# Gate and up of a shared expert: 32 products of 256 columns against 56 of 128 columns in the two-by-two scheme of the routed bases

## The chip, the cores and the metric

The kernel runs on one core of one Trainium2 chip. The metric is device time in microseconds (us). One execution was also taken with the hardware profiler; the page and the views of the trace that are quoted below all come from that one execution.

## The reference, cut to what matters

Eight batches of 256 tokens and 512 channels go through a layer norm and a windowed attention, and then, after a second layer norm (`xt`), through this block:

```python
gate = (xt @ w_gate).reshape(T, K, I)          # K = 8 bases, I = 256
up = (xt @ w_up).reshape(T, K, I)
basis = silu(gate) * up
...                                            # router: top 4 of 128 experts
mixed = einsum('tek,tki->tei', mix_sel, basis)
down = einsum('tei,ih->teh', mixed, w_down)
out = einsum('teh,te->th', down, coeff)
shared = silu(xt @ shared_w_gate) * (xt @ shared_w_up) @ shared_w_down
out = out + shared                             # shared_w_gate, shared_w_up: 512 x 512
```

Everything is f32. The routed part comes to a weighted sum over the 8 bases with one weight per token and basis, followed by one product with `w_down`. The shared expert has 512 hidden units, as many as two bases, and no weight per token.

## The kernel before

**One list per engine.** The kernel is one program of Python generators (`project`, `attention`, `tail`, `feed_forward`), each working on one batch. A planner, `run` (L1110), always resumes the generator with the lowest due time. What a generator issues between two yields goes to the engines' queues in that order, and the number that it yields, times a length divided by its `total`, is its next due time. So the yields only fix the order in which instructions stand in each engine's queue; the time comes from the chip. Due times are counted in batches: `feed_forward(b)` runs from b to b+1 with `total=73.2` (L1146), `attention(b+2)` begins at b+0.8 (L1141), and `tail(b+1, 1)`, the last part of the next batch's attention and its router, starts at about b+0.64.

**Routed bases: seven products.** For each basis k gate and up are computed together. The tokens are split in two halves of 128 (t = 0, 1) and the 512 channels in two halves of 256, and instead of eight products of blocks seven are made of sums of blocks (Winograd's form of Strassen's scheme). The sums of tokens, `sT`, are four vector additions per batch in `token_sums` (L717), called by the tail of that batch as soon as its `hT` (the normed tokens, transposed) is whole. The sums of weights are made in batch 0 by `sub` (L838), stored to DRAM scratch by `keep` (L846) and loaded in place of the originals from batch 1 on. `block(k, m, dst)` (L887) is one of the seven products: two matmul calls, tokens as the stationary operand (128x128), weights moving with 256 columns.

**One basis in the queues.** `one_and_five` (4 calls), then `first_tile` of the basis before (an addition `up0` on VectorE, a tanh on ScalarE, `silu2` on VectorE), `four` of the basis before (2 calls), copies `u` and `m5` on ScalarE, `mix_product` (VectorE, with an addition on GpSimd), `seven_and_six` (4 calls), `second_gate` of the basis before (addition `gate1`, tanh, `silu2`), `two_and_three` (4 calls), and `keep_seven` (a copy on ScalarE, an addition on VectorE, two on GpSimd). Three PSUM banks rotate among all of these (`next_bank`, L79).

**Shared expert.** After basis 7 (L1007 to L1057) gate and up are made as plain products with the weights standing still: for each of four blocks `ic` of 128 hidden units, 4 calls for gate and 4 for up, 256 tokens moving, into one bank `ps`; then a tanh, `silu2` and one product give `shT[:, ic, :]`, transposed as the down product needs it. The 8 calls of L1025 for `ic` = 0 are interleaved with what is left of basis 7; after `ic` = 2 the mixture is transposed (`pm`, four transposes) and copied to `mT` on ScalarE (L1060).

**Down products.** 12 calls of 512 columns: four with the lower half of the shared hidden units (L1071), and per tile of tokens two with `mT` and two with the upper half (L1088); then `x = pd * tg + x` on VectorE (L1090) and a store.

**Loads.** All loads of weights are issued by SyncE (SP), whose queue is in order. `after(i, g)` (L340) asks for the piece two ahead once a buffer has been read. The pieces 8 and 9 are the shared weights, 8 loads of 256 KB in place of a base's 7. The tag `w30` holds the moving weights of product 7, and at the end of a batch the lower half of `sw_down` (`load_down`, L336); the `w30` pieces of the next batch's first two bases are loaded after the products of L1071 (L1075). The upper half of `sw_down` stays in SBUF as `later["sd"]` (L261). `diagonals` (L444) issues 16 DMAs per batch through SP.

In f32 each matmul call leaves two LDWEIGHTS rows (PEld) and two MATMUL rows (PE) in the trace, so the 256 calls of L1025 show as x512.

Of the kernel before, what the change touches and what calls it, by code (L numbers as in the profile page):

```python
# [9 lines left out]
F32 = mybir.dt.float32  # L10
I32 = mybir.dt.int32
AF = mybir.ActivationFunctionType
ALU = mybir.AluOpType
AX = mybir.AxisListType

P = 128
# [13 lines left out]
SI = 512  # L30
# [6 lines left out]
def gated_block(  # L37
# [79 lines left out]
    def weight(src, rows, cols, name, eng):  # L117
        t = const.tile([P, rows // P, cols], F32, tag=name, name=name)
        eng.dma_start(t, src.rearrange("(c p) n -> p c n", p=P))
        return t  # L120
# [131 lines left out]
    def first_weights():  # L252

        for k in (2, 3, 0, 1):
            for g in range(1, 5):
                load_gu(k, g)
            if k == 2:
                yield 1.0
                later["wd"] = weight(w_down, I, HID, "wd", nc.sync)

                later["sd"] = weight(sw_down[SI // 2 :], SI // 2, HID, "sd", nc.sync)  # L261
            if k == 3:
                yield 2.0
                yield from first_sums(2)
                yield 1.0
                yield from first_sums(3)
        yield 3.0
        yield from first_sums(0)
        yield 1.0
        yield from first_sums(1)  # L270
# [16 lines left out]
    def coefficients(amp, escale):  # L287
# [21 lines left out]
    HALF = HID // 2  # L309
    scratch = {  # L310
        (k, g): sums.tile([P, 2, I], F32, tag=f"s{k}_{g}", name=f"s{k}_{g}")
        for k in range(NK)
        for g in range(1, 5)
    }

# [2 lines left out]
    def load_gu(i, g):  # L318

        b, k = divmod(i, PIECES)  # L320
        if b >= B or (k >= NK and g > 2):
            return
        wgu[i, g] = ts = [
            two.tile([P, 2, I], F32, tag=f"w{g}{j}", name=f"w{g}{j}_{i}")
            for j in range(1 if g == 3 else 2)
        ]
        if k >= NK:
            for half in range(2):
                nc.sync.dma_start(ts[half], (sw_gate if g == 1 else sw_up)[k - NK, half])
            return  # L330
        if g != 3 or k not in summed:
            nc.sync.dma_start(ts[0], (w_gate, w_gate, w_up, w_up)[g - 1][k, int(g in (2, 4))])
        if k in summed:
            nc.sync.dma_start(ts[-1], scratch[k, g])

# [4 lines left out]
    def after(i, g):  # L340

        b, k = divmod(i, PIECES)
        if g < 3:
            load_gu(i + 2, g)
        elif k < NK - 2:
            load_gu(i + 2, g)
        elif g == 3:
            load_down(b, k - (NK - 2))
        else:
            load_gu((b + 1) * PIECES + k - NK + 2, g)  # L350

# [360 lines left out]

    sides = {}

    def token_sums(b, hT):  # L717


        sT = one.tile([P, NC, T], F32, tag="sT", name=f"sT_{b}").rearrange(  # L720
            "p s (c n) -> p s c n", n=P
        )
        a11, a12 = hT[:, : NC // 2, :P], hT[:, NC // 2 :, :P]
        a21, a22 = hT[:, : NC // 2, P:], hT[:, NC // 2 :, P:]
        nc.vector.tensor_add(sT[:, 0], a21, a22)
        nc.vector.tensor_sub(sT[:, 1], sT[:, 0], a11)
        nc.vector.tensor_sub(sT[:, 2], a11, a21)
        nc.vector.tensor_sub(sT[:, 3], a12, sT[:, 1])
        return sT

    def tail(b, t, oT):
# [47 lines left out]
        give_bank()  # L779
        yield 2.5  # L780
        turned.add((b, t))
        if t == NT - 1:
            sides[b] = token_sums(b, hT)


        yield from take_bank()
# [76 lines left out]
    def feed_forward(b):  # L863
# [23 lines left out]
        def block(k, m, dst, first=False):  # L887
            g, j = weights_of[m]
            w = wgu[b * PIECES + k, g][j]
            for c in range(NC // 2):  # L890
                nc.tensor.matmul(  # L891
                    dst, lhsT=sides_of[m][c], rhs=w[:, c, :],
                    start=(first and c == 0), stop=(c == NC // 2 - 1), skip_group_check=True,
                )

# [58 lines left out]
        def mix_product(k, t):  # L956

            th, up = ths.pop((k, t)), tiles.pop(("m7" if t else "up0", k))
            nc.vector.scalar_tensor_tensor(  # L959
                out=th if k else mixed[t], in0=th, scalar=coef[b, t][:, k : k + 1], in1=up,  # L960
                op0=ALU.mult, op1=ALU.mult,
            )
            if k:
                nc.gpsimd.tensor_add(mixed[t], mixed[t], th)  # L964

        for k in range(NK):
            late = b == 0 and k > 3
            more = b == 0 and 3 < k + 1 < NK  # L970
            one_and_five(k)
            if late:
                keep(k, 3)
# [30 lines left out]
                keep(k + 1, 1)  # L1004


        i = b * PIECES + NK  # L1007
        shT = one.tile([P, NSI, T], F32, tag="shT", name=f"shT_{b}")

        def act(ic, pg):  # L1010
            th = tanh(pg[:, 0, :], f"sth_{b}_{ic}")
            yield 0.7
            silu2(th, pg[:, 0, :])
            nc.vector.scalar_tensor_tensor(
                out=shT[:, ic, :], in0=th, scalar=0.5, in1=pg[:, 1, :],
                op0=ALU.mult, op1=ALU.mult,
            )

        last = None
        for ic in range(NSI):  # L1020
            pg = next_bank(f"ps_{b}_{ic}")
            for j in range(2):
                w = wgu[i + ic // 2, j + 1]
                for c in range(NC):
                    nc.tensor.matmul(  # L1025
                        pg[:, j, :], lhsT=w[c // 2][:, c % 2, ic % 2 * P : (ic % 2 + 1) * P],
                        rhs=hT[:, c, :], start=(c == 0), stop=(c == NC - 1),
                    )
                if ic == 0:

                    if j == 0:
                        yield from first_tile(NK - 1)
                        yield 1.13
                        four(NK - 1)
                        mix_product(NK - 1, 0)
                        yield 0.86
                    else:
                        yield from second_gate(NK - 1)
                        yield 0.63
            if ic % 2:  # L1040
                for g in range(1, 3):
                    after(i + ic // 2, g)
            cost = 3.46 if ic > 0 else 0.0
            if last is not None:
                yield from act(*last)
                cost -= 0.7
            last = ic, pg
            if ic == 1:
                mix_product(NK - 1, 1)
            yield cost  # L1050
            if ic == 2:

                pm = next_bank(f"pm_{b}").rearrange("p t (j n) -> p t j n", j=2)
                for t in range(NT):
                    for j in range(2):
                        nc.tensor.transpose(
                            pm[:, t, j, :], mixed[t][:, j * P : (j + 1) * P], ident  # L1057
                        )
        mT = one.tile([P, NT, 2, P], F32, tag="mT", name=f"mT_{b}")
        nc.scalar.copy(mT, pm)  # L1060
        late = act(*last)


        down = [wgu[b, "sd", ic].rearrange("p c n -> p (c n)") for ic in range(NSI // 2)]
        down += [later["sd"][:, ic, :] for ic in range(NSI // 2)]
        pds = []
        for t in range(NT):
            po = next_bank(f"pd_{b}_{t}").rearrange("p a n -> p (a n)")
            pds.append(po)
            for ic in range(NSI // 2):  # L1070
                nc.tensor.matmul(  # L1071
                    po, lhsT=shT[:, ic, t * P : (t + 1) * P], rhs=down[ic],
                    start=(ic == 0), stop=False,
                )
        for k in range(2):  # L1075
            load_gu((b + 1) * PIECES + k, 3)
        cost = 3.46
        for step in late:
            yield step
            cost -= step  # L1080
        yield cost
        for t, po in enumerate(pds):
            inner = [(mT[:, t, j, :], later["wd"][:, j, :]) for j in range(2)]
            inner += [
                (shT[:, ic, t * P : (t + 1) * P], down[ic]) for ic in range(NSI // 2, NSI)
            ]
            for j, (lhsT, rhs) in enumerate(inner):
                nc.tensor.matmul(po, lhsT=lhsT, rhs=rhs, start=False, stop=(j == len(inner) - 1))  # L1088
            yield 3.46
            nc.vector.scalar_tensor_tensor(  # L1090
                out=xt[:, t, :], in0=po, scalar=tg[:, 1:2], in1=xt[:, t, :],
                op0=ALU.mult, op1=ALU.add,
            )
            nc.sync.dma_start(out[b, t * P : (t + 1) * P, :], xt[:, t, :])
        stored.add(b)


# [24 lines left out]
    with tc.manual_schedule():  # L1122
# [14 lines left out]
        for b in range(B):  # L1137
# [5 lines left out]
                at = float(b)  # L1143
            else:
                start(attention(1), 0.74, at=max(at, FIRST), total=74.1)
            start(feed_forward(b), b + 1.0 - at, at=at, total=73.2)  # L1146
            if b + 2 < B:
                start(project(b + 2), 0.62, at=b + (0.01 if b > 0 else -0.06), total=60.0)
        run(float(B + 1))
# [39 lines left out]
```

## Time and profile before

| what | us |
|---|---|
| median of 3 runs | 1043.92 |
| lowest, highest | 1040.56, 1044.18 |
| profiled execution, its own time | 1039.71 |
| its span, first to last instruction | 1037.9 |

| engine | busy us | share of the span |
|---|---|---|
| PE (TensorE matmul) | 999.2 | 96% |
| PEld (weight loads, beside PE) | 793.6 | 76% |
| DVE (VectorE) | 582.1 | 56% |
| POOL (GpSimd) | 439.7 | 42% |
| ACT (ScalarE) | 420.5 | 41% |

The profiled execution lies 4.2 us under the median of the timed runs and 0.85 us under the fastest of them; 1.8 us of its time lie outside its span. A row of a group gives the mean duration of one instruction; matmuls are pipelined, so the duration of one is longer than its distance to the next. The chain of waits is better for that: it gives for each run of matmuls how long the engine was held. From batch 1 to batch 5 the batches follow each other every 123.6 to 124 us. The DMA engines' mean share over the span is 55.7% for the queue that SP feeds.

### The profile page before, as it was taken

To read this page: it belongs to the slowest core of one execution; us is meant where nothing else is said; L and a number is where in the kernel's file an instruction comes from. 1 tells how busy PE (TensorE), PEld (TensorE's weight loads), DVE (VectorE), ACT (ScalarE), POOL (GpSimd) and SP (SyncE) were. 2 spreads that over 40 slices of the span, in tenths; PEclk is the share of its full clock that TensorE was granted. 3 is DMA by queue.
4 is the path that set the end of the run, shared out by engine and by line. 5 is a ranking of instruction groups with operands and counts; after the bars stand their busy time and mean duration, and the time that the engine had idled before them with its cause. 6 is when DMAs were issued, how large, how long until landed. Compare 5 with 4: busy or idle time off the path is not lost.

```text
span 1037.9 us, 26745 instructions
## 1 busy us (share of the span) xinstructions
PE 999.2 (96%) x10072; PEld 793.6 (76%) x10072; DVE 582.1 (56%) x2185; ACT 420.5 (41%) x1608; POOL 439.7 (42%) x860
## 2 busy tenths in 40 slices
PE   6789989999999999999999999999999999999998
PEld 5657877867788688886878868787788868777885
DVE  1565666747554575536755467544756457754452
ACT  3452554426441464315543256423554136431220
POOL 3666456605542265413644136521454216540340
PEclk9889999999999999999999999999999999999999
DMA  8833964549543693527745386444954368553880
GB/s 254 217 109 115 234 186 150 174 129 283 163 137 111 169 300 123 159 98 191 263 138 157 107 235 217 144 136 125 278 163 144 112 166 258 167 174 120 263 277 20
DMA packets 111104, 180.80 MB, mean 174 GB/s; under 512 B 12160, under 2 KB 34176, under 8 KB 110976
## 3 DMA queue, kind: packets, MB, share of 16 engines
q1 hardware_dynamic: 108480, 176.22, 55.7%
q10 hardware_dynamic: 2112, 1.84, 0.5%
q8 instruction: 79, 1.29, 0.5%
q0 software_dynamic: 384, 1.05, 0.5%
q14 instruction: 49, 0.40, 0.1%
HBM read 149.69 MB, written 12.58 MB: 156 GB/s over the span
## 4 chain that ended last, share of the span: by engine, by line
PE 83%; DVE 8%; ACT 2%; DMA 2%; issue 2%; POOL 1%; SPq 1%; ACTq 0%; POOLq 0%; DVEq 0%
PE m L891 32%; PE ps L1025 10%; PE pq L512 8%; PE sc L645 5%; PE pd L1088 5%; PE po L758 5%; PE sc L576 5%; PE pd L1071 3%; PE pv L532 2%; PE pk L493 2%; DVE pr L589 2%; PE pl L789 1%; DVE pt L623 1%; ACT pr L603 1%; DMA w<-in_L_ffn_w_up 1%
## 5 line engine op out<-in xcount | busy, mean ns | idle before, releaser
L615 POOL TENSOR_SCALAR pr<-pr,rd 128x192 f32<-128x192 f32 (+2 forms) x512 | 206.5, 422 | 271.1 <-DVE rd L612 257.9
L603 ACT ACTIVATE pr<-pr,nm 128x192 f32<-128x192 f32 (+2 forms) x512 | 218.6, 430 | 109.8 <-DVE nm L589 73.8
L891 PE MATMUL m<-w,sT 128*128 128x256 f32 x1024 | 252.7, 381 | 0.1
L589 DVE CUSTOM_DVE_ANT_1 pr<-sc,nbias 128x192 f32<-128x192 f32 (+2 forms) x512 | 153.5, 322 | 122.9 <-PE sc L576 108.7
L891 PEld LDWEIGHTS m<-w,sT 128*128 128x128 f32 x1024 | 194.3, 191 | 27.7 <-issue 1.0
L891 PE MATMUL m<-w,hT 128*128 128x256 f32 x768 | 204.1, 388 | 0.0
L891 PEld LDWEIGHTS m<-w,hT 128*128 128x128 f32 x768 | 139.8, 191 | 24.2 <-issue 5.4
L964 POOL TENSOR_TENSOR mixed<-mixed,th 128x256 f32<-128x256 f32 x112 | 82.0, 732 | 177.3 <-DVE th L959 175.7
L1025 PE MATMUL ps<-hT,w 128*128 128x256 f32 x512 | 117.6, 381 | 0.0
L623 DVE STREAM_TRANSPOSE pt<-pr 128x768 f32<-128x768 f32 (+2 forms) x128 | 111.4, 871 | 3.3 <-POOL prob L798 1.9
L1025 PEld LDWEIGHTS ps<-hT,w 128*128 128x128 f32 x512 | 95.2, 190 | 14.7 <-issue 2.9
L603 ACT ACTIVATION_READ_ACCUMULATOR pr<-pr,nm 128x1 f32 x512 | 97.8, 191 | 0.0
L645 PEld LDWEIGHTS sc<-pt,vbd 64*32 64x32 f32 x5120 | 61.8, 106 | 27.5 <-issue 12.2
L645 PE MATMUL sc<-pt,vbd 64*32 64x96 f32 (+2 forms) x5120 | 70.9, 229 | 7.1 <-DMA vbd<-vpad 3.5
L576 PE MATMUL sc<-kT,qT 32*128 32x192 f32 (+2 forms) x1024 | 67.8, 343 | 6.3 <-DVE nm L589 6.0
L927 POOL TENSOR_TENSOR m<-m,u 128x256 f32<-128x256 f32 x64 | 47.7, 745 | 55.9 <-DVE u L926 47.0
L576 PEld LDWEIGHTS sc<-kT,qT 32*128 32x128 f32 x1024 | 48.2, 188 | 27.6 <-DVE nm L589 9.2
L949 DVE TENSOR_TENSOR gate<-u,m 128x256 f32<-128x256 f32 x64 | 26.4, 413 | 67.5 <-PE m L891 67.5
L854 ACT ACTIVATE th<-m 128x256 f32<-128x256 f32 x64 | 24.7, 386 | 96.6 <-DVE up L937 94.5
L854 ACT ACTIVATE th<-gate 128x256 f32<-128x256 f32 x64 | 26.5, 415 | 87.4 <-DVE gate L949 87.4
L758 PE MATMUL po<-wo,oT 128*128 128x512 f32 x128 | 57.7, 594 | 0.3 <-DVE cf L832 0.3
L512 PE MATMUL pq<-ctT,wq 128*128 128x256 f32 x224 | 54.2, 385 | 2.8 <-ACT kT L500 2.8
(129 smaller groups left out, 1212.8 us busy)
## 6 DMA issues: line engine op xcount, KB each, us to landing
w<-s SPq DMA_DIRECT2D x232, 256.0 KB, 3.3
w<-in_L_ffn_w_gate SPq DMA_DIRECT2D x132, 256.0 KB, 3.1
w<-in_L_ffn_w_up SPq DMA_DIRECT2D x74, 256.0 KB, 4.0
vbd<-vpad SPq DMA_DIRECT2D x120, 128.0 KB, 3.3
s<-w SPq DMA_DIRECT2D x32, 256.0 KB, 3.1
w<-in_L_ffn_shared_w_gate SPq DMA_DIRECT2D x32, 256.0 KB, 3.1
w<-in_L_ffn_shared_w_up SPq DMA_DIRECT2D x32, 256.0 KB, 2.9
ctT<-in_ctx SPq DMA_DIRECT2D x8, 512.0 KB, 5.7
```

Source lines behind the costliest of these rows:

```text
L512: nc.tensor.matmul(pq, lhsT=wq_sb[:, c, g * P : (g + 1) * P], rhs=(ctT if c < NC else xnT)[:, c % NC, :], start=(c == 0), stop=(c == 2 * N ...
L576: nc.tensor.matmul(seen(scs[p][:, j * COLS : (j + 1) * COLS], qb), lhsT=qT[rows, qb].rearrange("p g q -> p (g q)"), rhs=kT[rows, par, :, f ...
L589: nc.vector.tensor_tensor_reduce(out=part, in0=seen(scs[p][:, j * COLS : (j + 1) * COLS], qb0 + j), in1=bass.AP(tensor=bias.tensor, offset ...
L603: nc.scalar.activation(part, part, AF.Exp, bias=nmax, scale=-1.0, accum_out=den)
L615: nc.gpsimd.tensor_scalar(part, part, rden[:, p : p + 1], 1.0, op0=ALU.mult, op1=ALU.mult)
L623: nc.vector.transpose(pt[:, u % 4].rearrange("p c (s k) -> p (c s) k", s=2)[:, :, lo:], pr.rearrange("p c (s k) -> p (c s) k", s=2)[:, :, ...
L645: nc.tensor.matmul(scs[gp][32 * c : 32 * (c + 1), 2 * COLS + lo * Q : 2 * COLS + hi * Q], lhsT=vbd[rows, kb % (P // Q), kb // (P // Q) * 2 ...
L758: nc.tensor.matmul(po, lhsT=oT[:, ch // 2, ch % 2, t * P : (t + 1) * P], rhs=wo_sb[:, ch % 2, ch // 2, :], start=(ch == 0), stop=(ch == 3),)
L891: nc.tensor.matmul(dst, lhsT=sides_of[m][c], rhs=w[:, c, :], start=(first and c == 0), stop=(c == NC // 2 - 1), skip_group_check=True,)
L964: nc.gpsimd.tensor_add(mixed[t], mixed[t], th)
L1025: nc.tensor.matmul(pg[:, j, :], lhsT=w[c // 2][:, c % 2, ic % 2 * P : (ic % 2 + 1) * P], rhs=hT[:, c, :], start=(c == 0), stop=(c == NC - 1),)
L1088: nc.tensor.matmul(po, lhsT=lhsT, rhs=rhs, start=False, stop=(j == len(inner) - 1))
```

## The change

The shared expert's gate and up become two more bases, 8 and 9, in the same seven products, with the roles of the operands exchanged: weights stand still, tokens (or their sums) move with 128 columns, and the result is already transposed. A block is then 4 calls of 128 columns in place of 2 of 256. `mix_product` of these two writes `shT`. Their weight sums are made, stored and loaded as for the other bases. Each hidden block pair of a basis covers `ic` = 2(k-8) and 2(k-8)+1; so `w30` now takes the rows `ic` = 0 and 2 of `sw_down`, and `later["sd"]` the rows 1 and 3. Basis 9 keeps `sT` in use until its `two_and_three`, so `token_sums` of the next batch is asked for twice: by the tail, and by `feed_forward` once `two_and_three(9)` stands in the queue; the later of the two issues it. The down products are ordered anew around what is left of basis 9, and the two `w30` loads for the next batch are issued separately. `total` is 72.9.

```diff
-                later["sd"] = weight(sw_down[SI // 2 :], SI // 2, HID, "sd", nc.sync)
+                later["sd"] = sd = const.tile([P, NSI // 2, HID], F32, tag="sd", name="sd")
+                nc.sync.dma_start(
+                    sd, sw_down.rearrange("(j o p) n -> o p j n", o=2, p=P)[1]
+                )
...
-        for k in range(NK)
+        for k in range(PIECES)
...
-        if k >= NK:
-            for half in range(2):
-                nc.sync.dma_start(ts[half], (sw_gate if g == 1 else sw_up)[k - NK, half])
-            return
         if g != 3 or k not in summed:
-            nc.sync.dma_start(ts[0], (w_gate, w_gate, w_up, w_up)[g - 1][k, int(g in (2, 4))])
+            of_bases, of_shared = ((w_gate, sw_gate), (w_up, sw_up))[(g - 1) // 2]
+            src = of_bases[k] if k < NK else of_shared[k - NK]
+            nc.sync.dma_start(ts[0], src[int(g in (2, 4))])
...
+        if g == 3 and k >= NK:
+            load_down(b, 2 * (k - NK))
+        else:
             load_gu(i + 2, g)
...
+    def token_sums(b):
+        if (b, NT - 1) in turned and (b == 0 or b - 1 in unsided):
+            sides[b] = sums_of_tokens(b, hTs[b])
...
+            if k < NK:
+                for c in range(NC // 2):
...
+                return
+            for ic in range(2):
+                cols = slice(ic * P, (ic + 1) * P)
+                for c in range(NC // 2):
+                    nc.tensor.matmul(
+                        dst[:, cols], lhsT=w[:, c, cols], rhs=sides_of[m][c],
+                        start=(first and ic == c == 0), stop=(c == NC // 2 - 1),
+                        skip_group_check=True,
+                    )
...
+            if k >= NK:
+                nc.vector.scalar_tensor_tensor(
+                    out=shT[:, 2 * (k - NK) : 2 * (k - NK) + 2, t * P : (t + 1) * P],
+                    in0=th.rearrange("p (c n) -> p c n", n=P), scalar=0.5,
+                    in1=up.rearrange("p (c n) -> p c n", n=P), op0=ALU.mult, op1=ALU.mult,
+                )
+                return
...
-        for k in range(NK):
+        for k in range(PIECES):
             late = b == 0 and k > 3
-            more = b == 0 and 3 < k + 1 < NK
+            more = b == 0 and 3 < k + 1 < PIECES
...
+        unsided.add(b)
+        token_sums(b + 1)
+        po0 = next_bank(f"pd_{b}_0").rearrange("p a n -> p (a n)")
+        for ic in range(2):
+            shared(po0, 0, ic, start=(ic == 0), stop=False)
+        yield from first_tile(last)
+        yield 1.13
+        four(last)
+        mix_product(last, 0)
+        yield 0.86
+        pm = next_bank(f"pm_{b}").rearrange("p t (j n) -> p t j n", j=2)
+        for t in range(NT):
+            for j in range(2):
+                nc.tensor.transpose(pm[:, t, j, :], mixed[t][:, j * P : (j + 1) * P], ident)
+        yield from second_gate(last)
+        mT = one.tile([P, NT, 2, P], F32, tag="mT", name=f"mT_{b}")
+        nc.scalar.copy(mT, pm)
+        shared(po0, 0, 3, start=False, stop=False)
+        yield 0.86
+        mix_product(last, 1)
+        for j in range(2):
+            mixture(po0, 0, j)
+        yield 1.73
+        shared(po0, 0, 2, start=False, stop=True)
+        po1 = next_bank(f"pd_{b}_1").rearrange("p a n -> p (a n)")
+        shared(po1, 1, 0, start=True, stop=False)
+        load_gu((b + 1) * PIECES, 3)
+        shared(po1, 1, 1, start=False, stop=False)
+        yield 2.6
+        put(po0, 0)
+        for j in range(2):
+            mixture(po1, 1, j)
+        yield 1.73
+        shared(po1, 1, 2, start=False, stop=False)
+        load_gu((b + 1) * PIECES + 1, 3)
+        shared(po1, 1, 3, start=False, stop=True)
+        yield 2.5
+        put(po1, 1)
...
-            start(feed_forward(b), b + 1.0 - at, at=at, total=73.2)
+            start(feed_forward(b), b + 1.0 - at, at=at, total=72.9)
```

`shared` is one down product of 512 columns with `shT[:, ic, ...]`, `mixture` one with `mT`, `put` the addition to `x` and the store (as L1090 and L1094).

## The prediction, on record before the change was run

> **What bounds the kernel.** I read the page first, then the chain of waits, then the timeline of one late batch. The chain, followed back from the last instruction, is almost all TensorE:
>
> ```profile
> PE 83%; DVE 8%; ACT 2%; DMA 2%; issue 2%; POOL 1%; SPq 1%; ACTq 0%; POOLq 0%; DVEq 0%
> PE m L891 32%; PE ps L1025 10%; PE pq L512 8%; PE sc L645 5%; PE pd L1088 5%; PE po L758 5%; PE sc L576 5%; PE pd L1071 3%; PE pv L532 2%; PE pk L493 2%; DVE pr L589 2%; PE pl L789 1%; DVE pt L623 1%; ACT pr L603 1%; DMA w<-in_L_ffn_w_up 1%
> ```
>
> So a shorter list of matmuls shortens the kernel, as long as no wait takes its place. What a matmul costs is not its mean duration (275 ns with 128 columns, 381 with 256: these overlap) but the time for which the chain is held by a run of them. The chain of waits of one batch (start, length, what, number of rows):
>
> ```profile
> 449.03 1.78 PE pv L532 x16
> ...
> 458.63 3.45 PE ps L1025 x16
> ...
> 470.89 0.89 PE pl L789 x8
> 471.78 3.44 PE pd L1071 x8
> ```
>
> One call leaves two rows. So a call with 256 columns (ps) holds TensorE for 3.45 / 8 = 0.431 us, one with 128 columns and a new stationary operand each time (pv) for 1.78 / 8 = 0.2225 (pl: 0.89 / 4, the same), one with 512 for 0.86. TensorE stands still for only about 1.1 us in a batch of 123.7.
>
> **The products.** Out: 32 calls x 0.431 = 13.80 us per batch. In: 2 bases x 7 products x 4 calls x 0.2225 = 12.46. The 12 down calls and 4 transposes stay. Saved: 1.34 us per batch, 10.7 over eight.
>
> [...]
>
> **Work off the path.** Two bases need on VectorE 2 x 3.1 us (407 + 413 + 414 + 413 + 439 + 2 x 505 ns) in place of 4 x 0.84, on ScalarE 2 x 1.92 in place of 4 x 0.38, on GpSimd 4 x 0.74 in place of nothing: 2.8, 2.3 and 2.9 us more per batch. It falls into the stretch where the shared expert stands now (busy time of PE, PEld, DVE, ACT, POOL; then clock, DMA share, GB/s):
>
> ```profile
> 447.00:455.00 8.00, 8.00 (x63) 7.47 (x53) 1.75 (x4) 1.88 (x6) 0.72 (x1) 1.00 0.32 113
> 455.00:462.00 7.00, 7.00 (x27) 4.65 (x26) 3.56 (x8) 0.38 (x1) 1.27 (x2) 1.00 0.16 49
> 462.00:471.00 9.00, 9.00 (x62) 7.84 (x61) 4.22 (x20) 3.54 (x13) 0.24 (x1) 1.00 0.37 126
> ```
>
> VectorE is busy for 9.5 of 24 us there, ScalarE for 5.8, the DMA engines for a third: hidden, also the 14 loads of 256 KB in place of 8 (1.5 MB more per batch, 3.0 us each to land). In batch 0 the sums of two more bases add 4 x 0.69 us on VectorE, 4 x 1.27 on GpSimd and 8 stores. The nearest row: the sums of bases 0 to 7 (L844) made their engines wait 9 us in all for loads, and TensorE waits for 1.3 us in the last 45 us of that batch. Bounds 0 and 2.6 us (two sums ahead of GpSimd's next work); I take 0.8.
>
> **Waits at the end of a batch.** From the yields and lengths I worked out the order in every queue. For batches 1 to 5, after the last product of `two_and_three(9)`, TensorE has: score (u=0), two shared products, the router's pl, `four(9)`, pm, shared(0,3), mixture, score (u=1), the other down products. VectorE: soften, `up0`, soften, `silu2`, the four token sums (b+0.8309), two softens, mix product, `gate1` (b+0.8536), soften, a reciprocal, the router's maximum rnm; ScalarE: prob (b+0.8602), the tanh of `gate1` (b+0.8605), the copy to `mT`. So the copy now stands behind prob, which waits for rnm, which stands behind `gate1`. Before, the copy came ahead of prob and had 3.44 us of L1071 to hide it. The pieces, as they lie in the batch before the change:
>
> ```profile
> 467.95 0.42 DVE L725 TENSOR_TENSOR sT<-hT 128x256 f32<-128x256 f32 x1
> ...
> 469.42 0.22 DVE L589 CUSTOM_DVE_ANT_1 pr<-sc,nbias 128x64 f32<-128x64 f32 x1
> ...
> 470.35 0.56 ACT L1060 COPY mT<-pm 128x512 f32<-128x512 f32 x1
> ...
> 472.14 0.28 DVE L795 TENSOR_REDUCE rnm<-pl 128x1 f32<-128x128 f32 x1
> ...
> 472.46 0.37 ACT L800 ACTIVATE prob<-pl,rnm 128x128 f32<-128x128 f32 x1 [1.14 <-DVE rnm L795]
> ```
>
> The sums take 469.42 - 467.95 = 1.47 us; rnm to prob is 0.32. Counted from the end of `two_and_three(9)`: TensorE reaches pm at 0.08 + 0.70 + 1.72 + 0.89 + 0.89 = 4.28 and the mixture at 4.28 + 0.44 + 0.86 = 5.58. VectorE: first soften 0.83, `up0` 0.98, soften 1.32; tanh on ScalarE 1.49 to 1.89; `silu2` 1.94, sums 2.28 to 3.75, softens, mix product 4.03, `gate1` 4.5 (`four` ends at 4.28), soften 4.84, reciprocal 5.06, rnm 5.2. ScalarE: prob 5.5, tanh 5.9, `mT` 6.3 to 6.85; the weight load of the mixture takes 0.2. **TensorE waits until 7.1: 1.5 us**, plus 0.1 at shared(0,3). Then `silu2` 6.4, soften, mix product 7.0, the router's top four 7.35 to 9.3 (2.0 us, as from 472.95 to 475.0), and the softens that free the banks of the next score at 9.3 and 9.5: that score, due at 8.8, ends **0.4 us** late. Bounds: with the tanh ahead of prob, 0.5 and nothing; with VectorE one stream transpose (0.97) later, 2.5 and 1.4.
>
> A wait also goes:
>
> ```profile
> 483.62 0.44 PE L576 MATMUL sc<-kT,qT 32*128 32x64 f32 x4
> 484.28 0.98 PE L576 MATMUL sc<-kT,qT 32*128 32x64 f32 x12 [0.22 <-DVE nm L589]
> ```
>
> The last score of a batch stands right behind the router's pc and waits for softens that stand behind its result; the first four rows are held 0.49 us too long. Now two down products (1.72 us) lie between. Nothing of this chain is late next: the softens are done by 15.3 on the scale above, the score comes at 16.4.
>
> Batches 1 to 5: -1.34 - 0.49 + 2.0 = +0.17 each, **+0.9**. Batch 6 has no scores, but the sums and the router's top four (2.05) stand ahead of mix product and `gate1`: shared(0,3) starts at 5.7 instead of 3.1, the mixture at 7.05 instead of 4.0; +3.0 - 1.34, **+1.7**. Batch 7: `four` ends 2.6, `gate1` 3.2, tanh 3.7, copy 4.3, mixture 4.5 instead of 3.9: **-0.7**. Batch 0: tanh ahead of the exponentials, 0.45; with 0.8 for the sums and the saving, **-0.1**. Sum: +1.8 us on the profiled 1039.71, or 1041.5. The median of the runs lies 4.2 higher, so I forecast 1043.92 + 1.8 = **1045.7**: even. A measurement of this kernel tells about 0.5% (5.2 us) from no change.
>
> One thing could make batch 6 dearer. After 2.09 us without work the next four rows took 2.05 us where they take 1.03 elsewhere:
>
> ```profile
> 920.97 0.51 PE L829 MATMUL pc<-mix,selT 128*128 128x8 f32 x2 [2.09 <-ACT selT L824]
> 921.34 2.05 PE L891 MATMUL m<-w,hT 128*128 128x256 f32 x4
> ```
>
> That is half speed, 1.7 us lost in all, once at most. [...]
>
> **The loads through SP.** The `w30` piece of the next batch's basis 0 waits for shared(1,0), and eight of the 16 `vbd` DMAs (10.69 us for 16 rows) now stand before it: SP gets through them by 10.6, shared(1,0) ends at 11.9, the piece lands at 15.3 (3.3 us), and product 7 needs it at 19.0. The second piece, behind the other eight and a store, lands by 21.5 and is needed at 25.2. Slack 3.7 us each: no cost.
>
> **Rivals.**
> - *The waits are hidden* (0.17): ScalarE and VectorE keep ahead, as everywhere else in this trace, where `mT` made TensorE wait 0.3 us in all. Then -10.7 - 5 x 0.5 = -13: 1031. Against it: the order of the queues.
> - *Half hidden* (0.15): 1.0 us per batch in place of 2.0, -1 in batch 6: 1.8 - 5 - 1: 1040.
> - *Slower: the late loads* (0.17). Between batches the DMA engines are busiest (0.92 of the first 12 us of a batch) and `w30` has one buffer per parity. It decides once a piece lands over 3.7 us after my figure, for instance if the `vbd` DMAs wait for the batch's own store or landing doubles. Then product 7 of bases 0 and 1 waits, by 0.7 us if landing goes from 3.3 to 7.7, by 2 if SP is held one product longer: 7 x 0.7 to 7 x 2 on top, 1051 to 1060.
> - *Weight loads bind* (0.03): at 190 ns a row 112 of them are 21.3 us per batch, 7.5 more than before, 1100. pv and pl, which load as often, exclude it nearly.
> - *Even* (0.48): 1040 to 1050.
>
> **How the numbers follow.** Faster by over 0.5%: the hidden case, two thirds of the half hidden, a little of the even: 0.30. Slower: late loads, weight loads, a little of the even: 0.22. Same: 0.48. The range 1031 to 1056 takes in the hidden case and the lower half of the late loads.
>
> **What would show it.** Right: 16 rows of the new bases hold TensorE for 1.78 us; `mT` starts after prob in batches 1 to 5; TensorE idles 1 to 2 us before the mixture; the wait before the last score is gone; SP's `w30` loads land before product 7 asks. Wrong: `mT` ahead of prob, idle time at product 7, or 128 columns at over 0.246 us a call, where the saving is nothing.

## The result and the profile after

The changed kernel takes 1038.84 us, the median of 8 runs (1036.65 to 1042.54), beside 1041.86 for 8 runs of the kernel before (1038.31 to 1044.18): a ratio of 0.9982, with a 95% interval of 0.9963 to 1.0002 (the quotient of the two medians is 0.9971, inside it). That is no difference that this measurement can tell. The forecast was even, 1045.7 us; 3.9 of the 6.9 us between it and 1038.84 are the loss of 1.8 that was expected plus the 2.1 by which the median of the kernel before came down with more runs, and the remaining 3.0 are what the kernel gained by the medians (1.9 by the ratio).

The profiled execution of the kernel after took 1039.15 us, with a span of 1037.4 (before: 1039.71 and 1037.9). Its chain of waits, by engine and by line:

```profile
PE 79%; DVE 9%; DMA 4%; ACT 3%; POOL 2%; issue 2%; SPq 1%; ACTq 0%; POOLq 0%; DVEq 0%
PE m L896 31%; PE m L905 9%; PE pq L510 8%; PE sc L643 5%; PE po L763 5%; PE pd L1039 5%; PE sc L574 4%; PE pk L491 3%; PE pv L530 2%; PE pd L1042 2%; DVE pr L587 2%; PE pl L793 1%; DMA vbd<-vpad 1%; ACT pr L601 1%; POOL w L848 1%
```

The line of the old shared products (ps, 10%) is gone and the new blocks (m L905) have 9%. TensorE's share fell from 83 to 79 all the same: other engines now stand in the chain. Where the time went is seen by batch. The table takes the end of the second addition to `x` of each batch from the trace; "to the first product" ends at the first routed product (us).

| kernel | to the first product | rest of batch 0 | 1 | 2 | 3 | 4 | 5 | 6 | 7 |
|---|---|---|---|---|---|---|---|---|---|
| before | 102.85 | 134.76 | 123.88 | 123.68 | 123.56 | 123.59 | 123.62 | 106.16 | 72.90 |
| after | 104.81 | 134.67 | 123.67 | 123.43 | 123.43 | 124.41 | 123.87 | 103.58 | 72.05 |

The first column holds the same TensorE rows in every kernel; over the eleven profiled executions of this case it goes from 102.85 to 106.61. Of its 1.96 us here 1.63 lie in one run of rows, the first 32 of the queries (pq): 3.84 us before, at full granted clock, and 5.47 after, where a stretch at half clock lies over them (11.94 to 15.36). Both profiled executions of the old products have a short start (102.85, 102.91), and of the nine with the new ones one has (103.03), so the change doesn't force the longer one; whether it has a share in the rest isn't shown. Batches 1 to 5 are longer by 0.1 us on the mean, batch 6 is 2.6 shorter, batch 7 0.85. The table is of one execution per kernel; verdicts on whole kernels go by the timed runs.

**The products.** In the chain of waits of batch 3 of the kernel after (start, length, what, rows):

```profile
452.12 1.78 PE pv L530 x16
...
459.13 3.57 PE m L905 x32
```

32 rows are 16 calls, so a call of 128 columns holds TensorE for 0.223 us; 0.2225 had been taken. The saving of some 1.3 us per batch is real. Summed over a whole batch, from the start of each run of product rows to the start of what follows, routed and shared products together hold TensorE for 63.26 us where it was 64.27: 1.0 us, the switches to other work included.

**The end of the batch.** The timeline of the same batch, all engines (start, length, engine, line, operation, output and input; in brackets the idle time before and what ended it):

```profile
472.24 0.42 DVE L964 TENSOR_TENSOR gate<-u,m 128x256 f32<-128x256 f32 x1
...
472.88 0.26 DVE L799 TENSOR_REDUCE rnm<-pl 128x1 f32<-128x128 f32 x1
...
473.17 0.37 ACT L804 ACTIVATE prob<-pl,rnm 128x128 f32<-128x128 f32 x1 [0.72 <-DVE rnm L799]
...
473.53 0.41 ACT L858 ACTIVATE th<-gate 128x256 f32<-128x256 f32 x1
...
473.83 0.57 ACT L1070 COPY mT<-pm 128x512 f32<-128x512 f32 x1
...
474.46 1.98 PE L1042 MATMUL pd<-wd,mT 128*128 128x512 f32 x4 [0.96 <-ACT mT L1070]
...
476.37 0.59 PE L574 MATMUL sc<-kT,qT 32*128 32x192 f32 x4
...
477.28 1.12 PE L574 MATMUL sc<-kT,qT 32*128 32x192 f32 x12 [0.31 <-DVE nm L587]
...
478.33 2.84 PE L1039 MATMUL pd<-sd,shT 128*128 128x512 f32 x6
...
480.35 0.33 SPq L336 DMA_DIRECT2D w<-s  x1
480.73 5.31 SPq L447 DMA_DIRECT2D vbd<-vpad  x8
```

The order is the one worked out: `gate1` (gate), the router's maximum (rnm), prob, the tanh, the copy `mT`, and only then the mixture. By the distance to the usual start the mixture comes 1.13 us late: it follows shared(0,3) by 1.99 us (472.47 to 474.46, the first row from the same timeline), where one product holds TensorE for 0.86. The score holds TensorE for 1.96 us (476.37 to 478.33). In the kernel before it was one piece and held it for 1.17:

```profile
475.15 1.24 PE L576 MATMUL sc<-kT,qT 32*128 32x192 f32 x16
476.32 1.98 PE L1088 MATMUL pd<-wd,mT 128*128 128x512 f32 x4
```

So the score takes 0.79 us longer. The last score of the batch, whose rows had waited, is one piece now; to the next product it takes 0.65 us (484.88 to 485.53) where it took 1.57 (483.62 to 485.19):

```profile
484.88 0.73 PE L574 MATMUL sc<-kT,qT 32*128 32x64 f32 x16
```

### The profile page after: what moved, and what is told of

The parts are those of the page before. It is cut to its first block, busy times and chain, and to the rows that moved or that the text cites. A ratio compares the mean times of both kernels' runs of the same rounds, so it can differ in the third digit from the quotient of the medians.

```text
span 1037.4 us, 27827 instructions
## 1 busy us (share of the span) xinstructions
PE 990.9 (96%) x10456; PEld 795.2 (77%) x10456; DVE 601.5 (58%) x2237; ACT 442.0 (43%) x1656; POOL 470.7 (45%) x896
## 4 chain that ended last, share of the span: by engine, by line
PE 79%; DVE 9%; DMA 4%; ACT 3%; POOL 2%; issue 2%; SPq 1%; ACTq 0%; POOLq 0%; DVEq 0%
PE m L896 31%; PE m L905 9%; PE pq L510 8%; PE sc L643 5%; PE po L763 5%; PE pd L1039 5%; PE sc L574 4%; PE pk L491 3%; PE pv L530 2%; PE pd L1042 2%; DVE pr L587 2%; PE pl L793 1%; DMA vbd<-vpad 1%; ACT pr L601 1%; POOL w L848 1%
## 5 line engine op out<-in xcount | busy, mean ns | idle before, releaser
L613 POOL TENSOR_SCALAR pr<-pr,rd 128x192 f32<-128x192 f32 (+2 forms) x512 | 209.6, 427 | 245.9 <-DVE rd L610 245.4
L942 POOL TENSOR_TENSOR m<-m,u 128x256 f32<-128x256 f32 x80 | 59.9, 749 | 83.6 <-DVE u L941 76.0
L858 ACT ACTIVATE th<-m 128x256 f32<-128x256 f32 x80 | 30.9, 386 | 142.8 <-DVE up L952 140.7
L643 PEld LDWEIGHTS sc<-pt,vbd 64*32 64x32 f32 x5120 | 61.6, 107 | 27.5 <-issue 13.2
L643 PE MATMUL sc<-pt,vbd 64*32 64x96 f32 (+2 forms) x5120 | 70.4, 230 | 7.9 <-DMA vbd<-vpad 4.3
L858 ACT ACTIVATE th<-gate 128x256 f32<-128x256 f32 x80 | 33.2, 415 | 94.2 <-DVE gate L964 94.2
L952 DVE TENSOR_TENSOR up<-u,m 128x256 f32<-128x256 f32 x80 | 33.3, 416 | 67.0 <-PE m L896 42.2
L574 PEld LDWEIGHTS sc<-kT,qT 32*128 32x128 f32 x1024 | 46.1, 188 | 32.5 <-DVE nm L587 13.8
L964 DVE TENSOR_TENSOR gate<-u,m 128x256 f32<-128x256 f32 x80 | 33.2, 415 | 64.1 <-PE m L896 55.6
L905 PE MATMUL m<-sT,w 128*128 128x128 f32 x512 | 65.1, 275 | 0.0
L1039 PE MATMUL pd<-sd,shT 128*128 128x512 f32 x128 | 62.3, 610 | 1.6 <-DVE shT L975 1.6
L905 PEld LDWEIGHTS m<-sT,w 128*128 128x128 f32 x512 | 61.2, 192 | 0.2
```

The costliest lines, as they stand in the source:

```text
L574: nc.tensor.matmul(seen(scs[p][:, j * COLS : (j + 1) * COLS], qb), lhsT=qT[rows, qb].rearrange("p g q -> p (g q)"), rhs=kT[rows, par, :, f ...
L613: nc.gpsimd.tensor_scalar(part, part, rden[:, p : p + 1], 1.0, op0=ALU.mult, op1=ALU.mult)
L643: nc.tensor.matmul(scs[gp][32 * c : 32 * (c + 1), 2 * COLS + lo * Q : 2 * COLS + hi * Q], lhsT=vbd[rows, kb % (P // Q), kb // (P // Q) * 2 ...
L858: nc.scalar.activation(th, gate, AF.Tanh, scale=0.5)
L905: nc.tensor.matmul(dst[:, cols], lhsT=w[:, c, cols], rhs=sides_of[m][c], start=(first and ic == c == 0), stop=(c == NC // 2 - 1), skip_gro ...
L1039: nc.tensor.matmul(po, lhsT=shT[:, ic, t * P : (t + 1) * P], rhs=down[ic], **flags)
```

## The experiments

Nine kernels, each timed beside the kernel before on the same chip. The theory at the start: the products save 1.34 us per batch, the last score 0.49 more, and the two waits above give it back; batch 6 is shorter for a reason of its own, the planner's new length. Batch lengths are read as in the table.

### The two waits

**The copy first.** The mixture's wait alone is taken away: the copy to `mT` is issued ahead of the tanh.

```diff
-        yield from second_gate(last)
         mT = one.tile([P, NT, 2, P], F32, tag="mT", name=f"mT_{b}")
         nc.scalar.copy(mT, pm)
+        yield from second_gate(last)
```

> The copy to mT is issued right after the four transposes, ahead of the tanh of gate1 and of the router's prob on ScalarE; nothing else changes. Theory (the saving of 1.34 us per batch is eaten by two waits on one chain, the mixture's for mT, 1.1 us, and the next score's for softens behind the router's top four, 0.9 us): the first wait goes, but the score then comes 1.1 us sooner and waits for the same softens, which have not moved, so in batches 1 to 5 the gain is given back; 0.3 us stay in each of batches 0, 6 and 7. Net -1 us, ratio to before 0.996 to 0.999. Rival (the waits are separate): -1.1 in five batches and -1, in all -6.5 us, ratio 0.992.

Measured: 1045.01 us, ratio 1.0039 [1.0019, 1.0059]; batches 1 to 5: 124.18, 123.80, 125.26, 126.12, 123.96. TensorE in batch 3:

```profile
476.17 1.96 PE L1042 MATMUL pd<-wd,mT 128*128 128x512 f32 x4
478.07 0.59 PE L574 MATMUL sc<-kT,qT 32*128 32x192 f32 x4
480.13 1.12 PE L574 MATMUL sc<-kT,qT 32*128 32x192 f32 x12 [1.47 <-DVE nm L587]
```

The mixture waits for nothing, and in the score right behind it TensorE is idle for 1.47 us in place of 0.31. The wait has moved, not gone: both are fed by one chain on VectorE and ScalarE, and the score needs its end. That the total got 6 us worse than the kernel after was not expected (0.996 to 0.999 had been); the section on the hardware comes back to it.

**The score later.** The score's wait alone is taken away: two numbers of the planner put three shared products ahead of the score.

```diff
         for j in range(2):
             mixture(po0, 0, j)
-        yield 1.73
+        yield 0.6
...
         shared(po1, 1, 1, start=False, stop=False)
-        yield 2.6
+        yield 3.73
```

> Three shared products (2.6 us) are put ahead of the score of u=1; the copy to mT stays where it is. Theory: the score's wait of 0.9 us goes, the mixture's 1.1 us stays: -0.9 x 5 = -4.5 us against the change, ratio to before 0.993 to 0.995. Rival (VectorE is short of time at the end of a batch, so any order waits): no gain, 0.998, the wait shows at another product.

Measured: 1038.55 us, 0.9988 [0.9969, 1.0006]; batches 122.97, 122.79, 122.75, 124.93, 123.05. Four of the five are 0.64 to 0.82 shorter than in the kernel after, near the 0.79 by which the score was longer; the mixture still waits 1.13. The whole time doesn't show it, and the ratio that was expected, 0.993 to 0.995, lies outside the interval: the gain is 0.7 per batch and not 0.9, batch 4 has a stall of 1.96 us of its own (below), and the interval is 3.9 us wide.

**Both.**

> Both edits: mT copied first, and the three shared products ahead of the score. Theory: both waits go, -2.0 x 5 - 1 = -11 us against the change, and batches 1 to 5 follow each other every 121.8 us (before 123.7): ratio to before 0.987 to 0.990. If the sum of the two edits is much more than their sum taken one by one, the two waits lie on one chain. Rival: 0.993 or more.

Measured: 1029.90 us, 0.9904 [0.9880, 0.9929]; batches 121.80, 121.67, 121.51, 121.68, 121.94. Timeline of batch 3:

```profile
474.47 0.58 ACT L1069 COPY mT<-pm 128x512 f32<-128x512 f32 x1 [0.22 <-PE pm L1067]
474.97 0.37 ACT L804 ACTIVATE prob<-pl,rnm 128x128 f32<-128x128 f32 x1
...
475.13 1.96 PE L1042 MATMUL pd<-wd,mT 128*128 128x512 f32 x4
...
479.60 0.93 PE L574 MATMUL sc<-kT,qT 32*128 32x192 f32 x16
```

The copy stands ahead of prob, the mixture follows without idle time and the score is one piece of 16 rows. The batches are 1.95 us shorter than before the change, against 1.34 + 0.49 = 1.83 for the terms of the prediction that were savings. So the saving was there all along, and the two waits had eaten it. With the two edits taken singly beside it, this is the experiment that settles batches 1 to 5.

**The copy first, and one shared product ahead of the score** (half of the second edit, on top of the first).

```diff
-        yield 1.73
+        yield 0.6
         shared(po0, 0, 2, start=False, stop=True)
+        yield 1.13
```

> The copy to mT first, as in the run that came out slower, and one shared product (0.86 us) put ahead of the score. In that run TensorE stood still for 1.47 us before the score, and the clock fell to half for 3.4 us in three batches. Theory: with 0.6 us of idle time the clock doesn't fall, so the gain is more than the 0.86 us per batch taken from the wait: -4.3 us and some 5 more, ratio to before 0.994 to 0.996 against 1.004. Rival (the slower time had another cause than the clock): -4.3 us alone, 0.999 to 1.000.

Measured: 1035.00 us, 0.9933 [0.9909, 0.9956]; batches 123.03, 122.86, 122.57, 122.59, 122.72. One product of 0.86 us takes 1.9 us on the mean off the five batches of the copy-first kernel, and the whole time falls by 10 us. Most of the surplus lies with the clock: in the two batches of the copy-first kernel with a stretch at half clock, 3 and 4, the difference is 2.7 and 3.5 us (0.75 of the latter is a stall, below), in the other three 0.9 to 1.2.

### The last sums of tokens and batch 6

**The sums late.** Both edits, and the sums of tokens of the next batch issued after four more shared products.

```diff
-        unsided.add(b)
-        token_sums(b + 1)
...
         shared(po1, 1, 1, start=False, stop=False)
+        unsided.add(b)
+        token_sums(b + 1)
         yield 3.73
```

> As with both edits, and the four token sums of the next batch come after the shared products instead of right after two_and_three(9) or the tail. Theory: in batches 1 to 5 they cost nothing where they are (gate1 waits for four(9), not for them), so nothing changes; in batch 6 they stand ahead of up0 and delay the chain by 1.5 us, and without them TensorE's longest wait there falls under 1 us and the half clock after it goes (1.7 us): -1.5 to -3 us against both edits, ratio to before 0.985 to 0.988. Rival (the sums do cost in every batch): -1 x 5 more, 0.982.

Measured: 1026.82 us (1024.29 to 1028.61), 0.9868 [0.9841, 0.9895]; batches 121.65, 121.73, 121.74, 123.32, 122.05, then 100.56 and 71.67. Batch 6 is 3.2 us shorter than with both edits alone, and the wait at shared(0,3) went from 1.75 to 0.87 us, with no half clock after it. Of all kernels here this is the fastest one that does the whole work: its slowest run, 1028.61, is under the fastest with both edits alone, 1029.14, on the same chip, though the two intervals overlap.

**The planner's length alone**, in both directions: the kernel after with the old `total`, and the kernel before with the new one.

```diff
-            start(feed_forward(b), b + 1.0 - at, at=at, total=72.9)
+            start(feed_forward(b), b + 1.0 - at, at=at, total=73.2)
```

> The changed kernel with total=73.2, the planner's length of before; no work is added or left out. In batch 6 the order on VectorE turns back: gate1 of basis 5 ahead of the router's top four. Theory (batch 6 came out 2.6 us shorter in place of 1.7 longer because of that one swap): the wait of 2.1 us before the router's pc and the half clock after it come back, +3 us in batch 6. In batches 1 to 5 the tanh of gate1 comes ahead of prob, but mT still behind it: the mixture waits 0.4 us less and the score 0.4 more, nothing net. Ratio to before 1.000 to 1.002. Rival (batch 6 is shorter because its products are fewer and lie otherwise): 0.998 as the changed kernel.

> The kernel before with total=72.9 and nothing else of the change. Theory: the swap in batch 6 alone takes the wait before pc from 2.1 to 0.6 us and the half clock with it, -3 us, batches 1 to 5 as before: ratio 0.996 to 0.998. Rival: 1.000.

Measured: the kernel after with 73.2 takes 1039.13 us, 0.9986 [0.9968, 1.0005]; the kernel before with 72.9 takes 1037.27, 0.9964 [0.9945, 0.9984]. In the first the time can't be told from the kernel after (1.000 to 1.002 had been expected, 0.998 was the rival's), in the second it is a small gain. The profiles are clearer. Batch 6 takes 106.32 us in the kernel after with 73.2 and 102.66 in the kernel before with 72.9 (before: 106.16; after: 103.58). The router's pc of batch 7, ahead of which TensorE had been idle for 2.09 us before the change, in the kernel after, in the kernel before with 72.9, and in the kernel after with 73.2:

```profile
920.35 0.39 PE L833 MATMUL pc<-mix,selT 128*128 128x8 f32 x2 [0.61 <-ACT selT L828]
```
```profile
916.41 0.39 PE L829 MATMUL pc<-mix,selT 128*128 128x8 f32 x2 [0.63 <-ACT selT L824]
```
```profile
922.45 0.39 PE L833 MATMUL pc<-mix,selT 128*128 128x8 f32 x2 [2.09 <-ACT selT L828]
```

The wait goes with the number and not with the products. At 73.2 `gate1` of basis 5 is due at 6.5195 of a batch, just ahead of the router's top four at 6.5204; at 72.9 it is due at 6.5217, behind it. With the old order `gate1` waits at the head of VectorE's queue for TensorE's next product while the top four, which pc needs, stand behind; in the kernel after with 73.2:

```profile
914.98 0.42 DVE L964 TENSOR_TENSOR gate<-u,m 128x256 f32<-128x256 f32 x1 [2.40 <-PE m L896]
```

A second wait of TensorE in batch 6, some 20 us earlier, goes the same way: 1.52 us at 73.2 and 1.04 at 72.9, in both kernels.

The kernel after with 73.2 shows one thing more. In its batch 3 the tanh falls ahead of prob:

```profile
474.14 0.42 ACT L858 ACTIVATE th<-gate 128x256 f32<-128x256 f32 x1 [0.16 <-DVE gate L964]
...
474.55 0.37 ACT L804 ACTIVATE prob<-pl,rnm 128x128 f32<-128x128 f32 x1
...
474.91 0.58 ACT L1070 COPY mT<-pm 128x512 f32<-128x512 f32 x1
...
475.54 1.98 PE L1042 MATMUL pd<-wd,mT 128*128 128x512 f32 x4 [0.66 <-ACT mT L1070]
...
477.45 1.50 PE L574 MATMUL sc<-kT,qT 32*128 32x192 f32 x16
```

The mixture is 0.82 us late, and the score, now without an idle piece, holds TensorE for 1.43 us to the next product, 0.26 over the kernel before. This is the order of the prediction's lower bound ("0.5 and nothing"), at a somewhat higher price, and its batches are 123.32, 123.25, 123.22, 124.80, 123.36: 0.2 to 0.5 us under the kernel after, but for batch 4 with its stall.

### The rivals

**The load late.** The kernel after, with the first `w30` load of the next batch behind all 16 `vbd` DMAs, for the rival of the late loads.

```diff
         shared(po1, 1, 0, start=True, stop=False)
-        load_gu((b + 1) * PIECES, 3)
         shared(po1, 1, 1, start=False, stop=False)
         yield 2.6
+        load_gu((b + 1) * PIECES, 3)
```

> The changed kernel, with the w30 piece of the next batch's basis 0 issued behind all 16 vbd DMAs in place of the first eight, 5.8 us later. The rival of the prediction was that this load comes late. Theory: in the changed kernel it lands about 3.6 us before product 7 asks for it (issued at 480.35, 3.4 us to land, asked for at 487.3), so product 7 of basis 0 now waits for 2.2 us in each of the batches after 0 to 5 (batch 6 has no vbd DMAs): +13 us against the change, ratio to before 1.010, a little more where the clock falls after the wait. If the slack were already gone: +5.8 x 6 = +35, ratio 1.03. If landing doesn't matter: no change.

Measured: 1042.44 us, 1.0007 [0.9982, 1.0032]; batches 124.26, 123.59, 123.68, 125.04, 123.33. A miss: 2.6 us over the kernel after by the ratios, with intervals that overlap, and not 13. SP's queue in batch 3 says why:

```profile
475.77 11.42 SPq L447 DMA_DIRECT2D vbd<-vpad  x16
...
487.29 0.55 SPq L336 DMA_DIRECT2D w<-s  x1
```

In the kernel after, SP stops in the middle of the `vbd` DMAs until shared(1,0) has been read. Without that stop it gets through all 16 at once; the load is issued only 3.8 us later on the scale of the batch (mixture to load: 9.71 in place of 5.89), and product 7 waits 0.29 us. The slack had been put at 3.7, and a load late by just that much costs nearly nothing. The rival was not the case, and the experiment's own expectation had left out that the moved load was itself what held the queue.

**Tokens standing still.** The sums-late kernel, with bases 8 and 9 made as the others are, two calls of 256 columns per block; `shT` is then laid out otherwise and the shared part of the output is not the reference's.

```diff
-            if k < NK:
+            if k < PIECES:
                 for c in range(NC // 2):
```

> The version with both edits and late sums, but bases 8 and 9 use the routed bases' form: tokens stand still, 14 calls of 256 columns per basis in place of 28 of 128. The products are left untransposed, so shT holds them in the wrong order and the shared expert's part of the output is not the reference's; all other work is the same. It measures what the standing weights cost by themselves. Theory: 28 x 0.2225 - 14 x 0.431 = 0.2 us per basis, 3.1 us over 16 bases: ratio to before 0.984 where the version itself has 0.987. Rival (many small products with 128 columns lose much more at the switches): 0.975 or less.

Measured: 1027.91 us, 0.9869 [0.9848, 0.9891]; batches 121.25, 121.26, 121.48, 121.68, 121.40. In batches 1, 2, 3 and 5 it is 0.26 to 0.65 us shorter than the sums-late kernel (batch 4 has a stall there; batch 6 is 0.77 longer, for a reason not looked into), near the 0.4 that 28 calls of 0.431 against 56 of 0.2225 make. Over a whole kernel that can't be told here, and the 0.984 that was expected was missed. So the price of the columns is nearly even: what the change saves is the eighth product (28 in place of 32 calls' worth), and the smaller calls cost 3%.

## Why the prediction was right, and where it was off

Even was right, for the reason given in five of eight batches, and partly by luck in the others.

- **The saving of the products** (1.34 us per batch): right. 0.223 us a call in the chain, 1.0 us by the whole batch, and 1.95 us per batch once both waits are gone, with the last score in it.
- **The wait at the mixture** (1.5 us, bounds 0.5 to 2.5): right in kind and place, 1.13 in size. The mixture came 6.6 us after the end of `two_and_three(9)` (467.84 to 474.46) and not 7.1: the copy was done at 6.56 where the list on paper had 6.85, and the mixture started 0.06 behind it where 0.25 had been allowed. The 0.1 at shared(0,3) did not come.
- **The score** (0.4): too small; 0.79 by its rows, 0.7 by the experiment that cures it alone. Both waits together are 1.9 where the sum had 2.0, so the split was off and not the total. That both waits hang on one chain was in the working; that curing one alone gives nothing was shown by the copy-first kernel.
- **The last score** (0.49 goes): right in kind, its 16 rows are one piece; too small in size. The 0.49 counted its first four rows alone, and the piece is shorter by 0.92.
- **Batches 1 to 5** (+0.17 each): by the measured terms -1.0 - 0.92 + 1.13 + 0.79 = 0.0. The five show -0.21, -0.25, -0.13, +0.82 and +0.25, +0.1 on the mean, with a stall of 0.64 in batch 4; no reason is known for the +0.25 of batch 5.
- **Batch 6** (+1.7): this term failed; it measured -2.6. The prediction's step was right by itself: `mix_product` and `gate1` do stand behind the sums and the top four, and TensorE is idle before shared(0,3), for 0.41 and 1.58 us in two pieces, with the half clock behind it that the prediction feared (from 950.61). What was left out was the change of `total` by 0.4%, which puts `gate1` of basis 5 behind the router's top four and takes away 1.5 of the 2.09 us of wait that the prediction quoted as a given, and the half clock behind it (from 921.10 before). With the old number batch 6 is at +0.16. On the new one, the products make +0.92 (102.66 to 103.58), still less than 1.7.
- **Batch 7** (-0.7): -0.85. **Batch 0** (-0.1): -0.09 behind the first routed product, from one execution each; its bounds were 0 and 2.6 us, and the kernel before with 72.9 had 132.40 for the same stretch, so this one is not better known than by 2 us.
- **No rival** was the case: nothing of the waits was hidden in the kernel as changed, the loads had slack, and the weight loads, at a mean of 192 ns a row, did not bind: a call still held TensorE for 0.223 us. The hidden case is what two moved lines and two planner numbers make of the change: 1029.90, where 1031 was given for it.

The luck: batch 6 came out 4.3 us better than its term, so that by the medians the kernel gained 3.0 us where a loss of 1.8 had been worked out; both are even.

What stays open: why the stall comes in some kernels and not in others, and how much of the difference between medians belongs to the start.

## What to carry over

Before a saving on the engine that bounds is counted, follow the chain that hands over at the end of the stage: here 1.83 us per batch were won and nearly all of it was given back at two waits fed by one chain, so both had to be moved before the whole time showed it. Where a planner orders the queues by numbers, work its order out again for the whole program when any constant changes, since two items 0.001 of a batch apart swapped and moved more time than the new products did in that batch. And where one chain feeds two waits of the bounding engine, cure them together: the cure of one alone made one long wait (1.47 us) out of two short ones here, and in two of five batches half clock followed the long one.

## What the runs showed of the hardware

**Half clock went with the busy share of a stretch, not with the length of a gap.** The traces record the granted clock by stretch. Every change to half clock in the eleven profiles starts on a grid of 3.413 us within its execution: in the kernel after at 46.08 and 950.61, which are 904.53 us or 265.0 steps apart, and the stretch that begins at 950.61 lasts one step, to 954.02. Two neighbouring stretches of the kernel before, the kernel after, and the kernel after with 73.2 (length, busy time of PE, PEld, DVE, ACT and POOL, then the granted clock, the DMA share and GB/s):

```profile
917.69:921.10 3.41, 1.32 (x7) 0.84 (x6) 2.69 (x7) 1.60 (x9) 2.50 (x4) 1.00 0.88 275
921.10:924.51 3.41, 3.41 (x10) 2.78 (x11) 1.75 (x4) 0.79 (x3) 2.08 (x5) 0.50 0.22 77
```
```profile
947.20:950.61 3.41, 1.42 (x9) 0.90 (x8) 2.77 (x13) 0.23 (x2) 0.00 (x0) 1.00 0.47 143
950.61:954.02 3.41, 3.41 (x6) 1.45 (x5) 0.85 (x2) 1.11 (x3) 0.00 (x0) 0.50 0.00 0
```
```profile
918.46:921.87 3.41, 1.90 (x9) 1.34 (x8) 3.09 (x11) 1.26 (x6) 1.80 (x3) 1.00 0.91 244
921.87:925.29 3.42, 2.84 (x14) 2.42 (x14) 2.43 (x6) 1.50 (x5) 2.81 (x6) 1.00 0.51 156
```

All three had TensorE idle for about 2 us. Where it was busy for 1.32 or 1.42 of the stretch the next one ran at half clock; where the same gap of 2.09 us lay across a boundary and 1.90 were busy, it didn't. Over all stretches of the eleven executions that begin after 110 us and of whose successor at least half lies in the span: 14 of 15 with TensorE busy for under half are followed by half clock, 4 of 9 between 0.5 and 0.6, none of 20 between 0.6 and 0.7, and one of 2900 above, which is the second half of a pair. So the busy share sorts the cases of these runs, but for those between 0.5 and 0.6, and the length of the gap alone doesn't. A stretch at half clock costs up to 1.7 us (my estimate: half of the 3.413 us that the record gives for one).

This explains most of the copy-first kernel: its wait of 1.47 us at each batch end left two stretches at 0.57 busy, at 601.9 and 728.2 us, and half clock followed in each; with one product of 0.86 us put between, no stretch of batches 1 to 6 was at half clock. Two such stretches are up to 3.4 us of the 4.5 by which batches 1 to 5 are longer in sum than in the kernel after.

**A stall without a releaser.** In batch 4 of six of the eleven kernels TensorE stops once, after the 44th of 56 rows of the values (L643), for 0.64 us at 621.7 in the kernel after, 1.96 at 621.4 with the score later and 1.46 at 616.2 with the sums late. The trace names no wait for it (the chain says "issue"). The kernel before, in both lengths, and those with both edits, with the score half and with tokens standing still don't have it.

No run shows its cause. What stands near it in the traces are the packets of one DMA queue. The page's queue q8, of kind "instruction", moves packets of 16 KB, 79 in the kernel before for 20144 rows of PE and PEld and 83 in the kernel after for 20912, about one per 250 rows. In all six kernels the stall ends 2.4 to 2.8 us after a packet of q8 began. With both edits the same row came 2.42 us after that packet and TensorE was idle for 0.01; with the score half it came 5.77 us after it and didn't wait. Whether the packet has a part in the stall was not tested.
